# A GNN layer on one Trainium2 core: the n gate's second half copied out of PSUM by ScalarE, and the first filter group recorded after the second pair's convolution

## The chip, the core and the metric

One core of one Trainium2 chip runs the whole program in one launch. The metric is the device time of one execution in microseconds; the figures compared are medians of several executions. TensorE (PE in the profile, with its weight loads as PEld) multiplies, VectorE (DVE) and ScalarE (ACT) do the elementwise work and empty PSUM, GpSimd (POOL) does a few small operations and issues some DMAs, and SyncE (SP) issues most DMAs. [...]

## What is computed

`x` is 64 graphs of 256 nodes with 256 channels, `adj` the 64 adjacency matrices. Every graph is normalised and passed through one gated layer with a residual. All is in float32. The reference, cut:

```python
h = jnp.maximum(_layernorm(x), 0.0)
# inside the layer, its x is h:
xc     = transpose(x)
c      = relu(bn1(conv1d(xc, conv1_w, 0)))            # one tap
c      = bn2(conv1d(c, conv2_w, 8))                   # 17 taps along the nodes
x_conv = transpose(relu(c + xc))
s      = x @ w_se.T + b_se                            # 3 numbers per node
A      = exp(-dist(s, s)) * adj
x_nmp  = A @ relu(x @ w_msg.T + b_msg)
gi = concat([x_conv, x_nmp]) @ w_ih.T + b_ih          # 512 -> 768: r, z, n
gh = x @ w_hh.T + b_hh                                # 256 -> 768: r, z, n
r, z = sigmoid(gi_r + gh_r), sigmoid(gi_z + gh_z)
n  = tanh(gi_n + r * gh_n)
out = x_input + (1 - z) * n + z * x
```

The two changed places are the last but two line (`n`), and the preparation of the filters of the 17-tap convolution, which is made once at the start.

## The kernel before

**Tiling.** Two graphs form a pair: a tile has 128 channels on the partitions and 2 x 256 nodes in the free dimension, and there are two such tiles (`dc` = 0, 1) for 256 channels. The 32 pairs are worked off in 8 blocks of 4 pairs. In a block, the 17-tap convolution of all 4 pairs is done in a transformed domain: `split` and `forward` transform on DVE, 47 products (`begin` and `complete`, with `product`) multiply each frequency by its filter on PE, and `branch_back`, `odd_back`, `q_back`, `p_back` and `join` transform back. Each product takes one filter tile of 256 KB, which SP loads from DRAM (`filt`) into one of nine slots (`wb`) by `load_kinds`. Then each pair i in turn goes through `gates(i)`, whose code the change touches.

**The gates.** Each of the two gate sets is computed by `seven`: a Strassen-like scheme with seven products per input. `seven(i, RZ, rz)` yields the r and z gates, `seven(i, NH, n)` the two halves of the n gate: the half 0 of a PSUM tile holds `gi_n`, the half 1 holds `gh_n`. `seven` takes two PSUM tiles, `A` and `E`, from the ring `acc` (two tiles of two banks), and one (`p5`) from the ring `aux` (four tiles of one bank). [...] As soon as `A` is complete `opened(0, A)` runs, and at the end `opened(1, E)`; for the n gate these are calls of `n(dc, p)`. The next user of the ring `acc` is the next `seven`, or, after the fourth pair of a block, the `begin(0)` and `begin(1)` of the next block.

`n(dc, p)` is this chain: ACT moves the half 1 of `p` with a bias to `gn`; DVE multiplies by `tr` (which holds tanh for r); DVE adds 0.5 of that to the half 0, read from PSUM; ACT takes tanh; three DVE operations and two ACT copies (to `back`) end it. The DVE operation that reads half 0 is the last reader of `p`, and the PSUM tile is free for the ring after it. `XNM[i]` (ring of two tiles, `xnm`) is the aggregated message of pair i, made by `aggregate(i)` and last read by the matmuls of `gates(i)`; `aggregate(i + 2)` writes the same tile again.

**The order.** Nothing of this is emitted at once. A `Recorder` takes every operation as a task with a cost, and `plan` lists them by engine: among the operations that could start first on an engine, it takes the one with the least due time (`late`, counted back from the order in which the matmuls were recorded). Every instruction of the program is emitted by one line, L371, so that the profile tells operations apart by tile names and not by line. Planning is done twice: for the start with the first part of block 0, and for all the rest. So an edit in one place can move operations elsewhere.

**The start.** The four pairs of block 0 are normalised, transposed (`transpose_h`), convolved with one tap (`conv1`) and split, one after another. Between them stand groups of filter preparation: `filter_steps(n)` takes the next n steps off a list, and each step (`filters`) is two matmuls of the taps with fixed points (`aux<-taps,points` or `acc<-taps,points` in the profile), an ACT copy and a DMA to `filt`. The taps come by DMA (`taps<-in_c_wT_dram`), in several parts. The first calls are `filter_steps((1, 2, 3, 3)[j])` after pair j.

**Other names.** `embed` transposes `z` (`aux<-ident,z`) and copies it to `zT`; `affinity` makes four small matmuls from it (`aux<-zT`, nine rows each, in four row groups of the array), takes exp on ACT to `e` and multiplies by `adj`. `message` is `aux<-w_msg,hT`. `finish` turns `back` by a DMA transpose to `gn`, and `deliver` adds x and writes the output (`out_dram<-back`, issued by POOL).

Of the kernel before, what the change touches and what calls it, by code (L numbers as in the profile page):

```python
# [16 lines left out]
ALU = mybir.AluOpType  # L17
# [469 lines left out]
def kernel(  # L487
# [18 lines left out]
    nc = Recorder(tc.nc)  # L506
# [91 lines left out]
    def chunk(t, g, c):  # L598
        return t[:, g * N + c * P:g * N + (c + 1) * P]
# [3 lines left out]
    X, ADJ, HT, XNM, STATS = {}, {}, {}, {}, {}  # L603
# [121 lines left out]
    p = aux()  # L725
# [3 lines left out]
    def columns(name):  # L729
        t, n = ROWS[name]  # L730
        k = sum(n)
        p = aux()
        nc.tensor.transpose(p[:, :k], t, ident[:k, :k])
        c = keep(f"{name}_columns", k)
        nc.vector.tensor_copy(c, p[:, :k])
        return [c[:, sum(n[:j]):sum(n[:j + 1])] for j in range(len(n))]
# [24 lines left out]
    def norm(i):  # L761
        stats(i)
        _, m, r, h = STATS[i]
        if i < PB:
            nc.vector.scalar_tensor_tensor(h, m[:, :, 0], -1.0, r, op0=ALU.mult, op1=ALU.mult)
        for j in range(G * MC):
            v = X[i][:, j, :]
            if i == PB or (i == 0 and j < MC):
                nc.vector.tensor_scalar(v, v, m[:, j, 0:1], r[:, j:j + 1], ALU.subtract, ALU.mult)
            else:  # L770
                nc.scalar.activation(v, v, AF.Identity, scale=r[:, j:j + 1], bias=h[:, j:j + 1])
        if i == 0:
            BEHIND[1, MC] = nc.last["vector"]
# [108 lines left out]
    def filters(p, m, g, eng):  # L882

        kinds = bank_points[m].shape[1]
        size = min(KG, P - g * KG)
        for dc in range(DC):
            mm(p[:size * kinds, dc * D:(dc + 1) * D], points[m][:size * TAPS, :size * kinds],
               taps[:size * TAPS, g, dc, :], start=dc == 0, stop=True, skip_group_check=True)
        t = taps[:, g].rearrange("p c o -> p (c o)") if m == len(PASSES) - 1 else evicted()
        nc.scalar.copy(t[:size * kinds], p[:size * kinds])  # L890
        if m < len(PASSES):
            eng.dma_start(
                out=filt[m][g * KG:g * KG + size].rearrange("k t c o -> (k t) (c o)"), in_=t[:size * kinds])
            return
        for k in range(size):
            for n, f in enumerate(filt):
                a = k * kinds + n * len(PASSES[0])
                nc.sync.dma_start(out=f[g * KG + k].rearrange("t c o -> t (c o)"), in_=t[a:a + f.shape[1]])
# [234 lines left out]
    def part(p, k, i, unit, start=False):  # L1133

        terms = [(half, gate, name) for name in ("h", "xn", "xc") for half, gate, names in unit if name in names]
        for n, (half, gate, name) in enumerate(terms):
            w, v = factors(k, i, gate, name)
            mm(p[:, half * N:(half + 1) * N], w, v, start=start and n == 0, stop=n >= len(terms) - 2,
               skip_group_check=True)
# [15 lines left out]
    def seven(i, unit, opened):  # L1155

        A = acc()
        part(A[:, 0], 1, i, unit, True)
        E = acc()
        nc.scalar.mul(E[:, 0], A[:, 0], -1.0)  # L1160
        p5 = aux()
        part(p5, 5, i, unit, True)
        e = slots[ROLE["e"]].rearrange("p c d -> p (c d)")
        nc.scalar.copy(e, p5)
        part(A[:, 0], 2, i, unit)
        part(E[:, 0], 6, i, unit)
        nc.vector.tensor_add(A[:, 1], E[:, 0], e)
        part(E[:, 0], 7, i, unit)
        nc.vector.scalar_tensor_tensor(E[:, 1], E[:, 0], -1.0, e, op0=ALU.mult, op1=ALU.subtract)
        part(A[:, 1], 3, i, unit)  # L1170
        opened(0, A)
        part(E[:, 0], 4, i, unit)
        opened(1, E)

    def halfs(p, k):
        return p[:, :, k * N:(k + 1) * N]

    def pieces(t):
        return t.rearrange("p (g n) -> p g n", n=N)

    def gates(i, between=None):
        tr, gn = tr_tile, gn_tile
        tz = [slots[ROLE[f"tz{dc}"]].rearrange("p c d -> p (c d)") for dc in range(DC)]

        def rz(dc, p):
            for gate, t in ((0, tr[:, dc]), (1, tz[dc])):
                nc.scalar.activation(pieces(t), halfs(p, gate), AF.Tanh,
                                     bias=b_rz[:, gate * DC + dc:gate * DC + dc + 1], scale=0.5 - dc)

        def n(dc, p):  # L1190
            g = gn[:, dc]
            nc.scalar.activation(pieces(g), halfs(p, 1), AF.Identity,
                                 bias=b_hh[:, 2 * DC + dc:2 * DC + dc + 1], scale=1.0 - 2 * dc)
            nc.vector.scalar_tensor_tensor(g, tr[:, dc], 1.0, g, op0=ALU.add, op1=ALU.mult)
            nc.vector.scalar_tensor_tensor(pieces(g), pieces(g), 0.5, halfs(p, 0), op0=ALU.mult,
                                           op1=ALU.subtract if dc else ALU.add)
            nc.scalar.activation(g, g, AF.Tanh, bias=b_ih[:, 2 * DC + dc:2 * DC + dc + 1])
            d = tr[:, dc]
            nc.vector.tensor_sub(d, HT[i][:, dc], g)
            nc.vector.scalar_tensor_tensor(d, tz[dc], 1.0, d, op0=ALU.add, op1=ALU.mult)  # L1200
            nc.vector.scalar_tensor_tensor(d, d, 0.5, g, op0=ALU.mult, op1=ALU.add)
            u = d.bitcast(U16).rearrange("p (n j) -> p j n", j=2)
            for j in range(2):
                nc.scalar.copy(back.bitcast(U16).rearrange("p (c j n) -> p c j n", c=DC, j=2)[:, dc, j], u[:, j])

        def last(dc, g, p):
            a = slice(g * N, (g + 1) * N)
            v, d = gn[:, dc, a], tr[:, dc, a]
            nc.scalar.activation(v, p[:, N:], AF.Identity,
                                 bias=b_hh[:, 2 * DC + dc:2 * DC + dc + 1], scale=1.0 - 2 * dc)  # L1210
            nc.vector.scalar_tensor_tensor(v, d, 1.0, v, op0=ALU.add, op1=ALU.mult)
            nc.vector.scalar_tensor_tensor(v, v, 0.5, p[:, :N], op0=ALU.mult, op1=ALU.subtract if dc else ALU.add)
            nc.scalar.activation(v, v, AF.Tanh, bias=b_ih[:, 2 * DC + dc:2 * DC + dc + 1])
            nc.vector.tensor_sub(d, HT[i][:, dc, a], v)
            nc.vector.scalar_tensor_tensor(d, tz[dc][:, a], 1.0, d, op0=ALU.add, op1=ALU.mult)
            for c in range(MC):
                t = chunk(y_last[:, dc], g, c).rearrange("p (b h) -> p h b", b=NW)
                u, w = (q[:, c * P:(c + 1) * P].rearrange("p (h b) -> p h b", b=NW) for q in (d, v))
                nc.vector.scalar_tensor_tensor(t, u, 0.5, w, op0=ALU.mult, op1=ALU.add)

        seven(i, RZ, rz)
        if between:
            between()
        if i + 1 < NP:
            seven(i, NH, n)
            return
        a0, p5, e1, a1, e0 = aux(), aux(), aux(), acc()[:, 1], acc()[:, 0]
        e = slots[ROLE["e"]].rearrange("p c d -> p (c d)")
        part(a0, 1, i, NH, True)
        nc.scalar.mul(e0, a0, -1.0)  # L1230
        part(p5, 5, i, NH, True)
        nc.scalar.copy(e, p5)
        part(a0, 2, i, NH)
        last(0, 0, a0)
        part(e0, 6, i, NH)
        nc.vector.tensor_add(a1, e0, e)
        part(e0, 7, i, NH)
        nc.vector.scalar_tensor_tensor(e1, e0, -1.0, e, op0=ALU.mult, op1=ALU.subtract)
        last(1, 1, e1)
        part(a1, 3, i, NH)  # L1240
        last(0, 1, a1)
        part(e0, 4, i, NH)
        last(1, 0, e0)
# [34 lines left out]
    def filter_steps(n, wide=True):  # L1278
        for _ in range(n):
            banks[0] += 1  # L1280
            p = acc()[:, 0] if wide and banks[0] % 3 == 0 else aux()
            filters(p, *steps.popleft(), nc.gpsimd if len(steps) % 2 else nc.sync)
# [9 lines left out]
    for j in range(PB):  # L1292
        if j > 0:
            norm(j)
        transpose_h(j)
        conv1(j, True)
        split(j)
        filter_steps((1, 2, 3, 3)[j])
    *bn2, b_ih, b_hh = columns("bn2")
    s2, h2_shift = fold_bn(bn2, "bn2", 1.0 / L)  # L1300
    b_rz = keep("b_rz", 2 * DC)
# [19 lines left out]
    for b in range(NB):  # L1321
        i = b * PB
# [91 lines left out]
        def between():  # L1414
            affinity(i + 2)
            join_h(nxt + 1)
            stats(nxt + 2)
# [106 lines left out]
```

## Time and profile before

| what | value |
|---|---|
| median of 3 executions | 1705.13 us (1702.14 to 1708.3) |
| the profiled execution | 1703.87 us |
| its span in the trace | 1702.1 us |
| granted TensorE clock | 0.994 |
| PE matmuls busy | 1666.3 us |
| DVE busy | 1457.8 us |
| ACT busy | 1052.4 us |
| POOL busy | 231.8 us |
| DMA traffic | 261.47 MB |

The profile is of one execution. A row of the timeline gives the start in us from the beginning of the span, how long the merged run of equal instructions took, the engine, the operation with the tile that it writes and those that it reads, its shape, how many were merged, and in brackets how long the engine was idle before it and what ended that. A float32 matmul is two instructions in the profile, so that x2 is one matmul of the code. `PEld` is a weight load, `SPq` the issue of a DMA by SyncE. A row of waits gives who waited for whom, the total in us, how many times, and the longest.

### The profile page before, as it was taken

Reading aid. Unit: us, or ns where it says so; the run is one execution under the profiler, and the core shown is the slowest. Engines: PE = TensorE matmul, PEld = TensorE weight load, DVE = VectorE, ACT = ScalarE, POOL = GpSimd, SP = SyncE. Lnnn points to the kernel's source line nnn. Section 1 sums busy time; section 2 is a strip of 40 time slices with the busy share of each in tenths; the row PEclk is TensorE's granted clock in tenths of the full one; section 3 lists DMA queues with packets and bytes.
Section 4 is the critical chain, followed back from the end, with each engine's and each line's share of the span. In section 5 each row is a group of like instructions: output and inputs, shape, how many; then the busy total and the mean of one; then the engine's idle time right before and its main releaser. Section 6 shows DMA issues by size and latency. Waiting matters only on the chain.

```text
span 1702.1 us, 26181 instructions
## 1 busy us (share of the span) xinstructions
PE 1666.3 (98%) x8984; PEld 1420.8 (83%) x8984; DVE 1457.8 (86%) x3401; ACT 1052.4 (62%) x1967; POOL 231.8 (14%) x245
## 2 busy tenths in 40 slices
PE   8999999999999999999999999999999999999998
PEld 5888878988889788888888887897888978898886
DVE  7969989799889998799997998979987899879545
ACT  5546665685657765676655866567575766556453
POOL 4211130022110121102110021101211012100010
PEclk9999999999999999999999999999999999999999
DMA  9982666966579366773559554694756836484032
GB/s 228 306 280 69 137 117 142 280 136 140 108 196 241 94 127 124 218 208 89 122 113 293 136 116 110 160 273 97 144 112 191 233 91 125 88 245 129 17 60 52
DMA packets 326812, 261.47 MB, mean 154 GB/s; under 512 B 204751, under 2 KB 252139, under 8 KB 326678
## 3 DMA queue, kind: packets, MB, share of 16 engines
q1 hardware_dynamic: 296982, 216.71, 48.4%
q0 software_dynamic: 29280, 42.76, 13.1%
q8 instruction: 71, 1.16, 0.3%
q14 instruction: 63, 0.52, 0.1%
q10 hardware_dynamic: 416, 0.32, 0.1%
HBM read 156.60 MB, written 43.78 MB: 118 GB/s over the span
## 4 chain that ended last, share of the span: by engine, by line
PE 77%; DVE 17%; DMA 3%; issue 1%; ACT 1%; SPq 0%; DVEq 0%; ACTq 0%
PE acc L371 52%; PE aux L371 25%; DVE V L371 3%; DVE T L371 3%; DVE U L371 2%; DVE gn L371 2%; DMA wb<-filt 2%; DVE tr L371 1%; DVE acc L371 1%; DVE wb L371 1%; DVE Yv L371 1%; DVE PT L371 1%; DMA taps<-in_c_wT_dram 1%; DVE msg L371 1%; DMA filt<-Yv 0%
## 5 line engine op out<-in xcount | busy, mean ns | idle before, releaser
L371 PE MATMUL acc<-wb,w_ih 128*128 128x256 f32 x768 | 191.9, 379 | 0.0
L371 PEld LDWEIGHTS acc<-wb,w_ih 128*128 128x128 f32 x768 | 145.9, 190 | 19.8
L371 POOL DMA_DIRECT2D back<-in_x_dram x62 | 61.9, 1161 | 696.6 <-ACT back L371 622.5
L371 POOL TENSOR_TENSOR rstd<-rstd,neg_half 128x4 f32<-128x4 f32 x32 | 81.6, 2548 | 472.7 <-DVE shift L371 284.8
L371 PE MATMUL aux<-wb,w_x 128*128 128x256 f32 x576 | 141.6, 384 | 0.6 <-ACT e L371 0.5
L371 DVE SCALAR_TENSOR_TENSOR V<-T,V 128x128 f32<-128x128 f32 (+2 forms) x448 | 140.2, 377 | 0.0
L371 PE MATMUL acc<-wb,w_x 128*128 128x256 f32 x576 | 136.5, 381 | 1.8 <-DVE acc L371 1.5
L371 PEld LDWEIGHTS acc<-wb,w_x 128*128 128x128 f32 x576 | 107.9, 190 | 28.6 <-DVE acc L371 8.4
L371 PEld LDWEIGHTS aux<-wb,w_x 128*128 128x128 f32 x576 | 108.0, 191 | 20.2 <-issue 4.0
L371 PE MATMUL aux<-w_msg,hT 128*128 128x259 f32 x512 | 120.9, 381 | 0.0
L371 PE MATMUL acc<-V,wb 128*128 128x128 f32 x1024 | 119.0, 275 | 0.6 <-ACT acc L371 0.6
L371 PEld LDWEIGHTS acc<-U,wb 128*128 128x128 f32 x1024 | 117.4, 192 | 1.5 <-issue 0.5
L371 PE MATMUL acc<-U,wb 128*128 128x128 f32 x1024 | 118.2, 275 | 0.3 <-DMA wb<-filt 0.3
L371 PEld LDWEIGHTS acc<-V,wb 128*128 128x128 f32 x1024 | 116.7, 192 | 1.2 <-ACT acc L371 0.8
L371 PE MATMUL acc<-wb,w_hh 128*128 128x256 f32 x384 | 110.1, 381 | 0.7 <-ACT acc L371 0.7
L371 DVE TENSOR_TENSOR T<-Yv 128x512 f32<-128x512 f32 (+1 forms) x80 | 42.5, 580 | 79.4 <-ACT Yv L371 78.9
L371 PE MATMUL aux<-hT,w_c 128*128 128x512 f32 x224 | 107.3, 595 | 2.7 <-ACT e L371 2.7
L371 PE MATMUL acc<-Yv,w_ih 128*128 128x256 f32 x380 | 108.5, 381 | 0.1
L371 PEld LDWEIGHTS aux<-w_msg,hT 128*128 128x128 f32 x512 | 96.5, 190 | 14.3
L371 PE MATMUL acc<-hT,w_hh 128*128 128x256 f32 x380 | 104.7, 383 | 0.6 <-ACT acc L371 0.4
L371 PE MATMUL acc<-xnm,w_ih 128*128 128x256 f32 x380 | 103.9, 380 | 0.0
L371 ACT COPY back<-gn 128x1024 uint16<-128x1024 uint16 x62 | 80.5, 1348 | 36.6 <-DMA gn<-back 36.6
(194 smaller groups left out, 3842.1 us busy)
## 6 DMA issues: line engine op xcount, KB each, us to landing
wb<-filt SPq DMA_DIRECT2D x376, 256.0 KB
back<-in_x_dram POOLq DMA_DIRECT2D x62, 256.0 KB, 7.3
out_dram<-back POOLq DMA_DIRECT2D x62, 256.0 KB, 4.8
x<-in_x_dram SPq DMA_DIRECT2D x58, 256.0 KB
halves_d<-halves SPq DMA_DIRECT2D x28, 512.0 KB
adjh<-halves_d SPq DMA_DIRECT2D x112, 128.0 KB
hh<-halves SPq DMA_DIRECT2D x108, 128.0 KB
filt<-Yv POOLq DMA_DIRECT2D x18, 224.0 KB, 4.6
```

The costliest lines, as they stand in the source:

```text
L371: self.tasks.append(Task(engine, lambda: method(*args, **kw), cost, size, self.first))
```

## The change

In `n(dc, p)` ACT copies the half 0 of the PSUM tile to SBUF right after it has moved the half 1. The copy goes into `XNM[i][:, dc]`, which the pair's matmuls have read by then, and DVE takes this operand from there. The function `last`, which serves the very last pair, is not changed. So 31 pairs have two more ACT copies of 128 x 512 each. In the start, the number of filter steps after pairs 0 to 3 goes from 1, 2, 3, 3 to 0, 2, 3, 4; their sum stays 9.

```diff
@@ in gates(i), n(dc, p) @@
             g = gn[:, dc]
             nc.scalar.activation(pieces(g), halfs(p, 1), AF.Identity,
                                  bias=b_hh[:, 2 * DC + dc:2 * DC + dc + 1], scale=1.0 - 2 * dc)
+            x = XNM[i][:, dc]
+            nc.scalar.copy(pieces(x), halfs(p, 0))
             nc.vector.scalar_tensor_tensor(g, tr[:, dc], 1.0, g, op0=ALU.add, op1=ALU.mult)
-            nc.vector.scalar_tensor_tensor(pieces(g), pieces(g), 0.5, halfs(p, 0), op0=ALU.mult,
-                                           op1=ALU.subtract if dc else ALU.add)
+            nc.vector.scalar_tensor_tensor(g, g, 0.5, x, op0=ALU.mult, op1=ALU.subtract if dc else ALU.add)
             nc.scalar.activation(g, g, AF.Tanh, bias=b_ih[:, 2 * DC + dc:2 * DC + dc + 1])
@@ at the start, for each pair j of block 0 @@
         conv1(j, True)
         split(j)
-        filter_steps((1, 2, 3, 3)[j])
+        filter_steps((0, 2, 3, 4)[j])
```

## The prediction

> **What bounds the kernel now.** I read the busy shares first, then the chain, then PE's own waits.
>
> ```profile
> PE 1666.3 (98%) x8984; PEld 1420.8 (83%) x8984; DVE 1457.8 (86%) x3401; ACT 1052.4 (62%) x1967; POOL 231.8 (14%) x245
> PE 77%; DVE 17%; DMA 3%; issue 1%; ACT 1%; SPq 0%; DVEq 0%; ACTq 0%
> ...
> PE acc L371 <- DVE tr L371: 9.4, 4, 2.4
> ...
> PE aux L371 <- ACT e L371: 3.2, 7, 0.5
> PE acc L371 <- DMA wb<-filt: 3.1, 4, 1.9
> PE aux L371 <- DMA taps<-in_c_wT_dram: 2.7, 1, 2.7
> ...
> PE acc L371 <- DVE gn L371: 1.8, 1, 1.8
> ```
>
> PE is the bound: 1702.1 - 1666.3 leaves 36 us in which it does nothing, so only waits of PE, and matmul time itself, can move the result. The largest group stands at the seven changes of block, where the first product of the next convolution (`acc<-Sv`) waits. In the timeline PE's gaps there are 1.75, 2.28, 1.95, 2.40, 2.36 and 2.36 us, and 0.24 + 0.58 at the last: 13.9 us, the most that this part of the change can win. One of them, all engines:
>
> ```profile
> 490.26 0.64 POOL L371 DMA_DIRECT2D out_dram<-back  x1 [4.19 <-DMA back<-in_x_dram]
> 490.52 11.63 SPq L371 DMA_DIRECT2D wb<-filt  x14
> ...
> 493.99 0.69 ACT L371 ACTIVATE gn<-acc,bn_columns 128x512 f32<-128x512 f32 x1 [0.61 <-PE acc L371]
> 494.29 0.68 DVE L371 SCALAR_TENSOR_TENSOR gn<-gn,acc 128x512 f32<-128x512 f32 x1
> ...
> 495.82 0.68 DVE L371 SCALAR_TENSOR_TENSOR gn<-gn,acc 128x512 f32<-128x512 f32 x1
> ...
> 497.11 3.81 PE L371 MATMUL acc<-Sv,wb 128*128 128x128 f32 x32 [2.28 <-DVE tr L371]
> ```
>
> PE ends at 494.82. DVE's reads of half 0 free tile A at 494.97 and E at 496.50. The label says `DVE tr`, but that operation does not touch the ring. The matmul also waits for its filter tile: in the trace's record of DMA completions the first `wb` load of this block is whole at 493.36, the second at 496.97, the third at 497.62, and the first product needs the second. So a DMA ends this wait, 0.5 us after PSUM was free and 2.0 us after A was. The same place one block later says so itself, and the stretch of the first shows the DMA engines full (second last but one figure, 1.02):
>
> ```profile
> 697.76 2.59 PE L371 MATMUL acc<-Sv,wb 128*128 128x128 f32 x11 [1.95 <-DMA wb<-filt]
> ```
> ```profile
> 494.60:497.10 2.50, 0.22 (x2) 0.03 (x1) 2.50 (x6) 1.88 (x7) 0.00 (x0) 1.00 1.02 318
> ```
>
> In the later blocks, too, the completion stands 0.13 us before PE's start (900.09 for 900.22, 1100.88 for 1101.01, 1301.66 for 1301.79). Two more places, the row-tiled matmuls and the start:
>
> ```profile
> 563.53 0.69 PE L371 MATMUL aux<-zT 9*128 9x256 f32 x2
> 570.40 0.71 PE L371 MATMUL aux<-zT 9*128 9x256 f32 x6
> 639.71 0.71 PE L371 MATMUL aux<-zT 9*128 9x256 f32 x8
> 640.88 1.13 PE L371 MATMUL aux<-hT,w_c 128*128 128x512 f32 x2 [0.45 <-ACT e L371]
> ```
> ```profile
> 14.67 0.60 PE L371 MATMUL aux<-taps,points 119*112 119x256 f32 x2
> 15.10 1.04 PE L371 MATMUL aux<-ident,T 128*128 128x128 f32 x8
> 18.82 2.02 PE L371 MATMUL aux<-taps,points 119*112 119x256 f32 x4 [2.68 <-DMA taps<-in_c_wT_dram]
> ```
>
> One, three or four `zT` matmuls in a row take the same 0.7 us (about 0.62 until the next can begin). And a group of four fills the four `aux` tiles, so that the next user of `aux` waits 0.45 us for the first exp.
>
> [...] the second load was issued 0.44 us after the first and landed 3.61 us later, beside POOL's `out_dram<-back`. [...] 677 ns for `gn<-gn,acc` out of PSUM, 681 for `gn<-tr,gn` out of SBUF. I count DVE at no change.
>
> **The change, part by part.** Sums are against the profiled execution, 1703.87 us (span 1702.1 and 1.8 around it); the median before, 1705.13, lies 1.3 higher. Positions come from comparing the order of each engine's instructions in the two built programs.
>
> *Copies on ACT.* 31 x 2 copies. The nearest rows, ACT copies of 128 x 512 out of PSUM (`acc<-acc` 575 ns, `wb<-aux` 584), give 0.58 each, 36 us in all, on an engine with 650 us idle. A is free at 493.38 + 0.58 = 493.96 instead of 494.97, E at 494.68 + 0.58 = 495.26 instead of 496.50. Queued behind the copies stand the two tanh of the n gate; they come 0.3 to 0.6 us later, and what follows them (`tr`, `back`, output) has 5 us and more to the next use. Cost on PE: 0 here.
>
> *The wait at the change of block.* PSUM comes free 1.0 to 1.2 us sooner, but the load doesn't: the slots are read, and the loads issued, at the same places as before, and the copies that lead to `out_dram<-back` keep their place against PE. In four of the blocks the changed order again begins with a product of the second load: gain 0. In one (the change at 497) it begins with the first load, in place since 493.36. That product (0.9 us) fits into the wait, but after three products PE meets the fifth tile to be read, landed at 499.58, where PE stands now at 499.8; only the two `z` transposes that slip in before it (0.45) and 0.1 are won: -0.55. First and last block: 0.
>
> *`zT` groups.* Before, the 32 groups of four stand in 46 runs, after in 49: each of four blocks has one run more (1+1+2 and 4 for 4 and 1+3), the end one less. 3 x 0.62 = +1.9.
>
> *Waits behind the groups.* In five blocks a single `zT` ahead of the third pair's group is joined to it, and `p5` (`aux<-wb,w_x`) follows at once: it waits for exp, 5 x 0.45. In four blocks the `aux<-hT,w_c` behind the fourth pair's group gives way to `acc` matmuls, -4 x 0.45; these then wait for DVE's `acc<-acc,wb`: 0.20 from the matmul + 0.69 + 0.05 against 0.62 of `zT` work, 4 x 0.3. Together +1.6. In the same five blocks an ACT copy `adj<-adjh` (1.35 us) moves ahead of `acc<-acc` of the third pair's n gate, and the matmul that follows is 0.4 late if nothing else delayed PE; the exp wait before may swallow it: 0 to 2.0, I take 1.0. In the last block, where DVE's `acc<-acc,wb` ends a wait of 0.74 at 1628, one more matmul has the same loop with less between: +0.3.
>
> *XNM.* `aggregate(i + 2)` can write the tile only after DVE has read it; in the new order its ACT copies stand behind the first tanh, and its PSUM tile is held 2 to 3 us longer. PE's rows there are other `acc` work, so 0; without that cover it would be 31 x 0.3, an estimate from the lag just worked out.
>
> *Filter steps.* The diff means to put the first step behind the second `conv1`. The built order doesn't: both taps matmuls of step 1 stand before it, since the planner takes what it believes ready. So PE still stops until the taps land at 18.69, and only steps 2 and 3 move behind `conv1`. PE's work up to 69 us stays the same. Two gaps of 0.4 and 0.3 us after 20.6 can go, one of about 0.5 can come where the fourth pair's transposes are copied on ACT: -0.7 to +0.5, I take 0. On SP `filt<-Yv` only changes place with `w_msg`. In the blocks SP issues `gn<-back` (3.5 us at 510.86) not between filter loads but some 33 us later; ACT needs it at 554.6, so 0.
>
> Sum: -0.55 + 1.9 + 1.6 + 1.0 + 0.3 = +4.2 us: 1708.1 on the profiled execution, and 1705.1 + 4.2 = 1709.3 on the median.
>
> **Rivals.** (a) The wait at the change of block does go, and the kernel is faster. For it: the PSUM release lies only 0.5 us before the load's end, and the DMA labels are few (4 in the table). If the second load landed before 495, by another interleaving with POOL's output, 6 gaps of 2.2 us would go: -13 + 4.2, about 1696. It decides from a second load more than 2 us earlier. Against it: nothing moves those transfers against PE. (b) ACT becomes the late one: with two more copies, PE loses one lag of 0.3 in each of 31 pairs, +9.3: 1718.6. For it: PE already waits on ACT and on ACT's DVE partners in every block. Against it: ACT at 64% has gaps of 1 to 4 us around the n gate. (c) The filter part does win its 2.7 us: 1706.6; against it stands the built order.
>
> **How the numbers follow.** A change under 0.3%, 5.1 us, can't be told from none in this kernel. My forecast and what lies within 3 us of it, (c) included: 0.68, of which about 0.42 stays within 0.3% and 0.26 passes it. (b): 0.20. (a): 0.12. So faster 0.12, same 0.42, slower 0.46. The range takes the unknown costs at their ends and the lower half of (b): 1702 to 1718.
>
> **What would show it.** Right: `acc<-Sv` at the changes of block still waits about 2 us, ended by `wb<-filt`; `aux<-wb,w_x` waits 0.45 for `ACT e` in five blocks; more `aux<-zT` runs; the 2.7 us for taps stays; ACT at 1088 us. Wrong: those first gaps under 1 us (a), or gaps of 0.3 us after each n gate (b).

## The result and the profile after

The changed kernel takes 1708.95 us (median of 20 executions, 1706.48 to 1714.93), the kernel before 1706.31 us on the same chip (20, 1702.14 to 1710.19). The ratio is 1.0025, with a 95% interval of 1.0015 to 1.0034: 2.6 to 5.8 us slower, 4.3 in the middle. This ratio, like all below, is the one that was recorded with its interval; the two medians themselves lie only 2.6 us apart (1.0015). The sum in the prediction was +4.2 us, which lies inside the interval.

The profiled execution took 1707.37 us, its span is 1705.6. From its page, the busy shares and the chain:

```profile
PE 1669.1 (98%) x8984; PEld 1421.7 (83%) x8984; DVE 1459.5 (86%) x3401; ACT 1079.0 (63%) x2029; POOL 243.9 (14%) x245
...
PE 76%; DVE 15%; DMA 6%; ACT 1%; issue 1%; SPq 1%; DVEq 0%; ACTq 0%
```

ACT has its copies (62 instructions and 27 us more); PE is the bound as before, and the share of DMA in the chain has gone from 3% to 6%. PE's waits (total us, times, longest):

```profile
PE acc L371 <- DMA wb<-filt: 12.1, 10, 2.4
PE aux L371 <- ACT e L371: 3.6, 8, 0.5
PE acc L371 <- DVE acc L371: 3.6, 8, 1.0
...
PE aux L371 <- DMA taps<-in_c_wT_dram: 1.8, 1, 1.8
...
PE acc L371 <- ACT xnm L371: 0.4, 1, 0.4
```

`DVE tr` and `DVE gn` are gone from the list, and it looks as if the copy had done its work. But `wb<-filt` has grown from 3.1 to 12.1 us, and 10.5 of these lie at the changes of block: the same stops under another name. The timeline of PE at two changes of block:

```profile
493.15 1.16 PE L371 MATMUL acc<-Sv,wb 128*128 128x128 f32 x8 [0.38 <-ACT xnm L371]
495.10 2.05 PE L371 MATMUL acc<-Sv,wb 128*128 128x128 f32 x16 [0.79 <-DMA wb<-filt]
496.99 0.38 PE L371 MATMUL aux<-ident,z 128*128 128x128 f32 x2
497.67 1.16 PE L371 MATMUL acc<-Sv,wb 128*128 128x128 f32 x8 [0.30 <-DMA wb<-filt]
...
895.80 1.04 PE L371 MATMUL aux<-w_msg,hT 128*128 128x259 f32 x4
899.20 3.11 PE L371 MATMUL acc<-Sv,wb 128*128 128x128 f32 x16 [2.37 <-DMA wb<-filt]
```

The first of them is the one place where the new order begins with the load that lands first: three short stops, 1.47 us in all, for one of 2.28 before. Its first label, `xnm`, is the new copy itself (`xnm<-acc`), which frees the PSUM tile. The next four stop as long as before (2.20, 2.37, 2.02, 2.25 us). Over all seven changes of block PE stood still for 13.9 us before and 12.5 after.

The places where the forecast expected new waits, in the timeline of the same kernel:

```profile
568.03 0.71 PE L371 MATMUL aux<-zT 9*128 9x256 f32 x8
569.20 0.70 PE L371 MATMUL aux<-wb,w_x 128*128 128x256 f32 x2 [0.45 <-ACT e L371]
...
637.83 0.71 PE L371 MATMUL aux<-zT 9*128 9x256 f32 x8
638.91 2.86 PE L371 MATMUL acc<-wb,w_x 128*128 128x256 f32 x12 [0.37 <-DVE acc L371]
```

At 569 the group of four stands together where before a single one and a group of three stood, and `p5` behind it waits for exp. At 639 the one-tap convolution that stood behind the group is gone, and `acc<-wb,w_x` waits for DVE. The first form comes in five blocks, the second in four.

### The profile page after: what moved, and what is told of

Read it like the earlier page. It is cut to its first block, busy times and chain, and to the rows that moved or that the text cites. A ratio compares the mean times of both kernels' runs of the same rounds, so it can differ in the third digit from the quotient of the medians.

```text
span 1705.6 us, 26240 instructions
## 1 busy us (share of the span) xinstructions
PE 1669.1 (98%) x8984; PEld 1421.7 (83%) x8984; DVE 1459.5 (86%) x3401; ACT 1079.0 (63%) x2029; POOL 243.9 (14%) x245
## 4 chain that ended last, share of the span: by engine, by line
PE 76%; DVE 15%; DMA 6%; ACT 1%; issue 1%; SPq 1%; DVEq 0%; ACTq 0%
PE acc L371 52%; PE aux L371 24%; DMA wb<-filt 3%; DVE V L371 3%; DVE tr L371 2%; DVE T L371 2%; DVE U L371 2%; DVE gn L371 2%; DMA x<-in_x_dram 1%; DVE acc L371 1%; DVE wb L371 1%; DMA taps<-in_c_wT_dram 1%; DMA halves<-hh 1%; DVE PT L371 1%; DVE st L371 1%
## 5 line engine op out<-in xcount | busy, mean ns | idle before, releaser
L371 POOL TENSOR_TENSOR rstd<-rstd,neg_half 128x4 f32<-128x4 f32 x32 | 87.7, 2740 | 457.8 <-DVE shift L371 278.0
L371 PEld LDWEIGHTS aux<-w_msg,hT 128*128 128x128 f32 x512 | 96.4, 190 | 14.3
L371 PE MATMUL aux<-e,msg 128*128 128x256 f32 x448 | 103.7, 379 | 0.0
```

The source lines that it names most:

```text
L371: self.tasks.append(Task(engine, lambda: method(*args, **kw), cost, size, self.first))
```

## The experiments

Each kernel ran five rounds beside the kernel before. All ratios are to the kernel before of the same chip, whose median was 1706.09 us for the first four of the table, 1705.16 for e_zt_a, e_zt_b, e_hold_b and e_hold_a, and 1706.17 for e_order_b, e_order_hold and e_hold_zt.

| kernel | median us | ratio | 95% interval |
|---|---|---|---|
| e_ngate: copy alone | 1711.41 | 1.0025 | 1.0012 to 1.0039 |
| e_filter: filter part alone | 1706.52 | 1.0005 | 0.9994 to 1.0017 |
| e_noout_b: before, without two writes a block | 1698.71 | 0.9951 | 0.9936 to 0.9965 |
| e_noout_a: changed, without them | 1697.07 | 0.9948 | 0.9928 to 0.9969 |
| e_zt_a: changed, zT groups together | 1705.39 | 1.0001 | 0.9989 to 1.0013 |
| e_zt_b: before, zT groups together | 1704.41 | 0.9992 | 0.9981 to 1.0003 |
| e_order_b: copy in the order of before | 1707.07 | 1.0009 | 0.9996 to 1.0023 |
| e_hold_b: before, writes moved | 1694.58 | 0.9939 | 0.9917 to 0.9960 |
| e_hold_a: changed, writes moved | 1700.31 | 0.9970 | 0.9956 to 0.9984 |
| e_order_hold: e_hold_b with the copy, order kept | 1694.54 | 0.9927 | 0.9909 to 0.9946 |
| e_hold_zt: e_hold_b, zT groups together | 1690.21 | 0.9912 | 0.9895 to 0.9930 |

### The two parts alone

```diff
 e_ngate, against the changed kernel:
-        filter_steps((0, 2, 3, 4)[j])
+        filter_steps((1, 2, 3, 3)[j])
 e_filter, against the kernel before:
-        filter_steps((1, 2, 3, 3)[j])
+        filter_steps((0, 2, 3, 4)[j])
```

In the two profiles the changed kernel stands 2.5 us ahead of the kernel before at 217 us and 3.5 behind at the end. I took that for a gain at the start.

> The copy in the n gate alone; the start prepares filters as before. Theory: in the profile of the changed kernel the start won about 2.8 us and the blocks lost about 6.3, so without the start's part the kernel is about 6 us slower than before (ratio 1.0035), with the offset against before near 0 up to 235 us, and 49 runs of zT matmuls. Rival: the start's gain was a chance of one execution and the blocks lose the forecast 4.2 us: ratio 1.0025, the same as the whole change.

> The filter part alone; the n gate reads PSUM as before. Theory: PE still stops for the taps until about 18 us, but the two gaps after 20.6 us and one of 0.6 us near 78 us go, so PE stands 2.5 to 3 us earlier at 133 us and the kernel ends 2.5 to 3 us earlier (ratio 0.9983 to 0.9985); the blocks keep their 46 runs of zT. Rival, the term of the forecast: nothing is won at the start, ratio 0.9995 to 1.0005.

Measured: 1.0025 and 1.0005. The interval of e_filter (0.9994 to 1.0017) leaves out the 0.9985 of my theory after the result, and the term of the forecast stands: the filter part wins 1 us at most. So the loss is that of the n gate, though the interval of e_ngate alone takes in both 1.0025 and 1.0035. The stretch of the first 45 us in each trace shows what had misled me; after the times of the five engines a line ends with the granted clock of PE, the DMA share and GB/s. Before, changed, copy alone, filter part alone, and the changed kernel without the writes:

```profile
0.00:45.00 45.00, 39.15 (x167) 26.85 (x168) 32.32 (x92) 24.17 (x44) 18.17 (x36) 0.96 0.97 231
```
```profile
0.00:45.00 45.00, 40.38 (x178) 28.22 (x179) 35.09 (x96) 25.64 (x46) 18.82 (x38) 1.00 1.00 245
```
```profile
0.00:45.00 45.00, 40.52 (x177) 28.76 (x178) 34.68 (x97) 25.64 (x46) 18.73 (x37) 1.00 0.98 242
```
```profile
0.00:45.00 45.00, 40.59 (x176) 28.83 (x177) 34.61 (x94) 25.53 (x46) 18.72 (x37) 1.00 0.99 243
```
```profile
0.00:45.00 45.00, 39.66 (x167) 26.82 (x168) 32.84 (x89) 24.31 (x44) 18.19 (x36) 0.96 0.97 232
```

The clock is 0.96 or 1.00, with the old start (first and third line) and with the new one (the others) alike. 0.04 of 45 us are 1.8 us. The missing clock is one piece: 3.4 us in which PE had half its clock, in the kernel before right behind the wait for the taps. The same 3.4 us, before and changed:

```profile
18.60:22.00 3.40, 3.18 (x6) 2.08 (x7) 1.66 (x3) 1.98 (x5) 1.02 (x4) 0.50 1.14 234
```
```profile
18.60:22.00 3.40, 3.40 (x9) 1.47 (x9) 2.11 (x4) 2.55 (x5) 1.02 (x4) 1.00 1.15 233
```

The wait for the taps stays in all five (1.8 to 2.7 us); in the eight traces with the old start it is anything from 0.3 to 3.0 us. In 13 traces the same matmul near 217 us (`acc<-hT,w_hh` behind an ACT copy) begins anywhere from 214.6 to 222.8 us: at 214.6 in the one that had no time at half clock until then, at 221.9 and 222.8 in the two that had the most, 17 us. The eight traces with the old start have a mean of 218.4, the five with the new one 217.8.

### The load at the change of block

These two leave out the writes of the output of the third pair of each block; every other instruction keeps its place on its engine.

```diff
-            nc.gpsimd.dma_start(out=rows(out, G * i + g), in_=row_tile(y, g))
+            k = nc.gpsimd.dma_start(out=rows(out, G * i + g), in_=row_tile(y, g))
+            if i % PB == 2:
+                nc.tasks[k].call = lambda: None
```

> The kernel before without the two writes of the output of the third pair of each block (that output is not written; every other instruction keeps its place). Theory: the second filter load of a block lands late [...]. Without them it lands within about 1 us of the first, and PE's gap at a change of block falls from 2.0 to 2.4 us to what DVE's read of PSUM allows, 0.3 to 0.6 us (tile free 0.15 us after PE's last matmul, and a lag): 6 gaps by 1.7, ratio about 0.994. Rival: the load is late because of its issue or of other transfers: the gaps stay above 1.5 us and the ratio above 0.998.

> The changed kernel without the same writes (that output is not written). Theory: with the load in time, the copy shows what it is worth: PSUM is free 0.9 us before PE's last matmul of the block, so the gaps at the changes of block fall under 0.2 us, 0.3 to 0.5 us less than in the kernel before without these writes, 6 times: the blocks' other losses of about 6 us stay, so the ratio to before is about 0.995, and it is still about 0.5 to 1 us slower than the kernel before without these writes (its start won 2.8). Rival: the gaps stay above 1.5 us.

Measured: 0.9951 and 0.9948. In e_noout_b the first two filter loads of the block at 494 us were issued at 490.27 and 490.70 and whole at 493.06 and 493.67: the second lands 0.6 us after the first, where it landed 3.6 us after it in the kernel before. So the writes held it up, by 3.0 us; by what path, neither trace shows. PE at the change of block, in the kernel before without the writes, and in the changed one without them:

```profile
493.53 1.04 PE L371 MATMUL aux<-w_msg,hT 128*128 128x259 f32 x4
494.82 2.92 PE L371 MATMUL acc<-Sv,wb 128*128 128x128 f32 x24 [0.25 <-issue]
```
```profile
698.15 1.04 PE L371 MATMUL aux<-w_msg,hT 128*128 128x259 f32 x4
699.02 1.16 PE L371 MATMUL acc<-Sv,wb 128*128 128x128 f32 x9
```

With the load in time the stop shrinks to 0.25 us without the copy (`acc <- issue`, 1.7 us in seven waits, is in PE's list there), and to nothing with it (but at 500 us, where the order differs, 0.38 for the copy `xnm` stay, and 5 us into the last convolution PE waits 2.35 us for a later load). That is the whole worth of the earlier release of PSUM: about 0.25 us at a change of block. The two kernels can't be told apart by their times. The forecast's rival (a) said what the changed kernel would take if the load came in time, about 1696 us; this kernel takes 1697.07.

A stop at a change of block can go with a further loss. Two blocks of the kernel before, with equal stops and the same work behind them, and the 3.4 us behind the first and the second stop:

```profile
1101.01 3.81 PE L371 MATMUL acc<-Sv,wb 128*128 128x128 f32 x32 [2.36 <-DVE tr L371]
1301.79 5.44 PE L371 MATMUL acc<-Sv,wb 128*128 128x128 f32 x32 [2.36 <-DVE tr L371]
```
```profile
1101.00:1104.40 3.40, 3.39 (x30) 3.40 (x31) 3.40 (x12) 1.18 (x3) 0.00 (x0) 1.00 0.93 330
1302.00:1305.40 3.40, 3.40 (x18) 3.40 (x18) 3.40 (x12) 0.39 (x1) 0.00 (x0) 0.50 0.77 272
```

At 1302 us the same 32 instructions take 1.6 us more, at half the clock (0.50 for 1.00). In the seven traces where the load is late, such a stretch comes at 11 of 39 stops of 1.6 us or more; in the six without the writes or with them moved it comes at no change of block (once, in e_noout_a, at the stop of 2.35 us just named). It comes with the kernel before and the changed one alike (twice in each of these profiles).

### The zT groups

The planner here lists the four matmuls of a group only when the `aux` tiles of all four are due. The tasks wait for nothing new on the chip.

```diff
+        waits = {k for t in turns for k in nc.tasks[t].preds if k < first}
+        for t in turns:
+            nc.tasks[t].preds |= waits
```

> The changed kernel, where the planner lists the four matmuls of a zT group only once all four aux tiles are due, so that they stand together: 42 runs of zT in place of 49 (before: 46), hardly anything else moves. Theory: a run costs PE 0.62 us whether it holds one matmul or four, so 7 runs less are 4.3 us less than the changed kernel: ratio to before 1.0000, the waits for ACT e stay. Rival: the runs are not what costs, since PE waits for the aux tiles or works elsewhere meanwhile: ratio 1.0025 as the changed kernel has.

> The same in the kernel before: 37 runs of zT in place of 46. Theory: 9 x 0.62 = 5.6 us less, ratio 0.9967. Rival: ratio 1.0000.

Measured: the changed kernel comes back to 1.0001, 4.1 us less, where 7 runs at 0.62 us are 4.3. In its last block 1.3 us came back as waits (2.1 for `ACT Yv` and 0.45 for `ACT e`, less 1.2 for `ACT zT`), so 3.0 would have been left; the intervals can't tell these apart. In the kernel before, 9 runs less bring 1.4 us (0.9992) and not 5.6. PE's waits in that kernel say where the rest went:

```profile
PE aux L371 <- ACT e L371: 5.9, 13, 0.5
...
PE acc L371 <- ACT Yv L371: 2.1, 1, 2.1
...
PE aux L371 <- DVE wb L371: 1.4, 6, 0.6
```

Before, `ACT e` had 3.2 us in 7 waits, and the other two were not there; a wait of 0.8 for `ACT zT` in the last block went. 2.7 + 2.1 + 1.4 - 0.8 = 5.4 us came back. In the five blocks where a single `zT` was joined to its group, `p5` now follows a group of four and waits 0.45 us. That is the step of the forecast by which the changed kernel loses at the same place, got here without any copy. So a run saved is worth its 0.62 us only where the work behind it doesn't wait for what the run makes.

### The copy without its order

Here the copy is put in behind the planner's back. The ACT task of half 1 also emits the copy, into a part of `Yv` that is dead by then, and the second DVE operation reads it there. Every other instruction stands where it stood.

```diff
+            x, move = xcv(i % PB, dc), nc.tasks[k].call
+
+            def both():
+                move()
+                tc.nc.scalar.copy(pieces(x), halfs(p, 0))
+            nc.tasks[k].call = both
```

> The same copies and the same second DVE operand from SBUF (into a part of Yv that is dead by then), but put in behind the planner's back: every other instruction of every engine stands as in the kernel before, with its 46 runs of zT; filter steps as before. Theory: the copy itself costs and wins nothing, since ACT has room and the filter load ends the wait at the change of block; all of the 4 us came from the order that the planner made of it: ratio 0.999 to 1.001, gaps at the changes of block still about 2.2 us. Rival: the copies cost by themselves, through ACT's queue: ratio 1.0025.

Measured: 1.0009. This is what the theory asked for, and 1.0025 lies outside the interval, though the interval meets that of e_ngate. The waits decide it:

```profile
PE acc L371 <- DMA wb<-filt: 14.0, 8, 2.4
...
PE aux L371 <- ACT e L371: 3.2, 7, 0.5
...
PE acc L371 <- DVE acc L371: 1.5, 3, 0.7
```

The second and the third line are those of the kernel before to the tenth. In the first, `DVE tr` 9.4, `DVE gn` 1.8 and `wb<-filt` 3.1 of before (14.3) have become one name with 14.0: nothing but the label changed.

### The writes moved, and what the copy is worth then

In these the two writes are issued by SyncE, and the planner lists them after the first loads of the next block (the edit in `plan` makes it count a predecessor that was recorded later). It puts them late in that block's convolution. All output is written. This order is planned anew too, with 42 runs of `zT` for 46, so the ratio is not that of the writes alone; e_noout_b, where nothing else moved, has 0.9951.

```diff
+            eng = nc.sync if i % PB == 2 else nc.gpsimd
-            nc.gpsimd.dma_start(out=rows(out, G * i + g), in_=row_tile(y, g))
+            k = eng.dma_start(out=rows(out, G * i + g), in_=row_tile(y, g))
+            if i % PB == 2:
+                HELD.append(k)
@@ at the end of a block @@
+        first = len(nc.tasks)
         load_kinds()
+        for n, k in enumerate(HELD):
+            if b + 1 < NB:
+                nc.tasks[k].preds.add(first + 1 + n)
+        HELD.clear()
@@ in plan @@
-            left[k] = sum(p in left for p in T[k].preds)
+            left[k] = sum(p in new for p in T[k].preds)
```

> The kernel before with the two output writes of the third pair of each block put on SyncE's queue behind the first filter loads of the next block (in the planned order they come late in that block's convolution, and the fourth pair's copies to back behind them; 42 runs of zT). All output is written. Theory: as without the writes, the six gaps at the changes of block go from 2.0-2.4 to under 0.7 us, about 10 us, and 4 runs of zT less are 2.5 us: ratio 0.992 to 0.994. Rival: the writes collide with other filter loads within the convolution, and PE waits there for as much: ratio above 0.998.

> The changed kernel with the same writes moved (41 runs of zT). Theory: with the loads in time the earlier release of PSUM takes 0.3 to 0.5 us more out of each of six changes of block, about 2 us, the five waits for ACT e cost about as much: within 0.001 of the kernel before with the writes moved. Rival: the copy costs 4 us in the blocks in any order: 0.0025 above it.

> The same copies, put in in the same way, in the kernel with the output writes moved, whose order stays as it is. Theory: now PSUM ends the wait at the change of block (0.25 us in five, 0.57 in one), and the copy takes that away: 1.5 to 2 us, ratio to before about 0.993 where the kernel with the writes moved has 0.994, and no wait for ACT of 1.1 us as in the changed kernel with the writes moved. Rival: ratio 0.997 as in that kernel.

> The kernel before with the output writes moved and the zT groups kept together: 37 runs in place of 42. Theory: 5 x 0.62 = 3.1 us less, of which the end of the last block gives back 2 (as the longer wait for the z transposes did there with the groups alone): ratio 0.993 to 0.9935. Rival: all of 3.1 counts: 0.992; or none, 0.994 and above.

Measured: e_hold_b 0.9939, as its theory had it. e_hold_a 0.9970, 0.0031 above it: there the rival won, but not through the copy itself. PE and then ACT in that kernel, in one of the five blocks that have it:

```profile
615.57 1.46 PE L371 MATMUL aux<-wb,w_x 128*128 128x256 f32 x6
618.17 0.70 PE L371 MATMUL acc<-hT,w_hh 128*128 128x256 f32 x2 [1.14 <-ACT acc L371]
```
```profile
615.58 0.67 ACT L371 ACTIVATE wb<-acc,b_rz 128x512 f32<-128x512 f32 x1
616.14 1.08 ACT L371 ACTIVATE hh<-x,shift,rstd 128x256 f32<-128x256 f32 x2
617.13 0.41 ACT L371 ACTIVATE z<-msg 128x12 f32<-128x12 f32 x3
617.45 0.19 ACT L371 COPY z<-msg 128x12 f32<-128x12 f32 x1
617.54 0.58 ACT L371 ACTIVATE acc<-acc 128x512 f32<-128x512 f32 x1
```

The `acc<-acc` for which PE waits stands behind two `hh` and four `z` operations, which in e_hold_b stand elsewhere or have an earlier start. And in e_hold_b PE has other work at this place, which e_hold_a does later:

```profile
617.13 1.02 PE L371 MATMUL aux<-hT,w_c 128*128 128x512 f32 x2
```

5 x 1.14 = 5.7 us; of the other waits, `ACT e` has 2.5 us more than in e_hold_b and `DVE acc` 2.2 less. The order was planned anew for the copy, and this is what came of it.

e_order_hold, the same copies in the order of e_hold_b, has none of these waits and takes 0.9927, which can't be told from e_hold_b (0.9939) but lies clear of e_hold_a: 0.9909 to 0.9946 with the order kept, 0.9956 to 0.9984 with a new one. (e_hold_a has the new start too, which e_filter showed to bring nothing.) PE at a change of block and later in the block, e_hold_b and then e_order_hold:

```profile
494.41 3.81 PE L371 MATMUL acc<-Sv,wb 128*128 128x128 f32 x32 [0.25 <-issue]
...
639.12 2.21 PE L371 MATMUL acc<-wb,w_x 128*128 128x256 f32 x9 [0.69 <-DVE acc L371]
```
```profile
498.89 1.04 PE L371 MATMUL aux<-w_msg,hT 128*128 128x259 f32 x4
499.76 3.81 PE L371 MATMUL acc<-Sv,wb 128*128 128x128 f32 x32
...
510.38 1.16 PE L371 MATMUL acc<-V,wb 128*128 128x128 f32 x8 [0.33 <-DMA wb<-filt]
...
644.76 1.56 PE L371 MATMUL acc<-wb,w_x 128*128 128x256 f32 x6 [0.92 <-DVE acc L371]
```

The 0.25 us at the change of block is gone in all six that had it, and so is the 0.57 at 295 us. But in four blocks the wait for DVE is 0.22 us longer: DVE works without a pause there and stands later against PE (its `acc<-acc,wb` begins 0.87 us after PE's `zT` at 643 us, where it begins 0.66 after it in e_hold_b). That the gate's DVE operations began later behind ACT's copies is the likely cause; no run isolates it. And PE, without the 0.25 us at the changes of block, meets more late loads (`wb<-filt` 5.2 us in 10 waits, where e_hold_b has 3.5 in 6). In these two profiles what the copy wins is given back.

e_hold_zt is the fastest, 0.9912, and beats both kernels, the kernel before by 12 to 18 us. I had expected 0.993 to 0.9935. The profile has 37 runs of `zT` for 42, and at the end of the last block the 2.1 us for `ACT Yv` that I had counted. Its interval takes in 0.993, so whether the groups brought more than their 1 to 3 us stays open.

## Why the prediction was right, step by step

- **The wait at the change of block, -0.55.** Right in its reason: the second load ends it, and the load is late because of POOL's writes. Taking the writes out removes the stop with or without the copy. In size it was -1.4 us in the profile of the changed kernel and -0.25 in that of the copy alone (13.65 us of stops).
- **The zT runs, +1.9.** 49 for 46 were counted. The price of 0.62 us is that of the timeline; e_zt_a's 4.1 us for 7 runs is in line with it but doesn't fix it, as said there.
- **The waits behind the groups, +1.6.** Five new waits of 0.45 for `ACT e`, four fewer ahead of `aux<-hT,w_c`, and four of 0.37 for DVE, where the forecast had 0.3: 2.26 - 1.81 + 1.48 = +1.9. In block 1 the same form grew as well (0.57 to 0.96 us at 236), which the forecast had not counted: +0.4.
- **The `adj<-adjh` copy, +1.0.** This term was mis-sized: nothing of it shows. It was the lower end of the bound (0 to 2.0). That the exp wait of 0.45 just before gives ACT the time is the likely cover; no run isolates it.
- **The last block, +0.3.** A new wait of 0.22 us, at 1647.3.
- **The filter steps, 0.** Right: 1.0005 alone. The built order kept both taps matmuls of step 1 ahead of `conv1`.
- **The copies on ACT, 0.** Right for the copies: put into the order of before they add no wait, and the 1.0009 can't be told from 1. ACT is busy 27 us more and not 36: a copy takes 0.58 us as forecast, but begins before the operation ahead of it has ended (at 491.22 us behind one that ends at 491.33). Rival (b), a lag in each of 31 pairs, shows nowhere.
- **DVE and XNM, 0.** Right: DVE's operation took 688 ns with both operands in SBUF (`gn<-gn,xnm`) and 677 with one in PSUM. PE stood idle 0.0 us ahead of `aux<-e,msg`, the matmuls of `aggregate`.

The terms as measured, without the filter part, are -0.25 + 1.9 + 1.9 + 0.4 + 0.2 = +4.2 us; e_ngate's 1.0025 is 4.3 (2.0 to 6.7). Waits for loads inside the convolutions are not in this sum: they were 0.5 us before, 1.6 in the changed kernel and 1.2 in e_order_b, in one profile each. That the sum on record was +4.2 too is partly luck: the 1.0 for `adj` that wasn't there stands against 0.3 (block changes), 0.3 (waits) and 0.4 (block 1) too little elsewhere. The forecast took a change under 0.3% for one that can't be told from none; with 20 executions of each kernel 0.25% could be told.

## What to carry to other kernels

Before a chain that frees a buffer is shortened, look up when everything else that the next instruction needs is there: the label of a wait names one of them, and another may be later and of quite another kind, here by 0.5 us a DMA that another queue's writes had held up by 3.0. Where a planner makes the order, an added instruction has two prices, its own (1.0009 here, which can't be told from 1) and that of the new order (1.0025 with both); putting it in with the order held fixed tells them apart. And two single profiles can differ by some us at the start for reasons that are not the change (one stretch at half clock was 1.8 of the first 45 us here), so a part of a change is judged by running it alone.

## What the runs showed of the hardware

- In these traces the granted clock of PE, where it is recorded, is 1.00 except in a few stretches of 3.4 or 6.8 us (longer at the end) at 0.50; in the kernel before they begin at 18.6, 697.9 and 1302.0 us (3.4 each) and at 1568.3 (6.8), the last at 1698.0. Up to 45 us there was none or one of them (clock 1.00, 0.96 or 0.92), from 90 to 290 us none to two (1.00 to 0.97), with no pattern by kernel that one profile of each could show. Those at the changes of block stand at stops of 1.95 to 2.51 us, but most stops of this length have none. What brings them was not tested.
- Two writes of 256 KB on POOL's queue together delayed the second of a row of 256 KB filter loads on SyncE's by 3.0 us (3.6 us after the first in the kernel before, 0.6 in e_noout_b, near 494 us), but not the first, which was whole 2.8 us after its issue both with and without them.
